# Selective scan: x_proj of a forward and its backward direction in one product, the result kept in DRAM, dt products contracted over all 108 rows

## The chip, the cores and the metric

The kernel runs on one core of one Trainium2 chip. The metric is the device time of one execution in microseconds; the time before is 4361.97 us, the median of three runs (4361.64 to 4367.63 us). The profile is one further execution, taken by the hardware profiler.

## The reference, cut to what matters

The model has two layers on an input of 4 images, 384 channels and 32 x 32 positions, all in fp32. Layer 0 is a selective scan (SSM) in four directions followed by a mixture of four experts, layer 1 is attention followed by a small feed-forward. The change touches the first lines of the scan alone:

```
xs = _cross_scan(x)          # k=0 rows, k=1 columns, k=2 rows reversed, k=3 columns reversed
x_dbl = einsum('bkdl,kcd->bkcl', xs, x_proj_weight)      # 44 x 384 for each k
dts, Bs, Cs = x_dbl[:, :, :12], x_dbl[:, :, 12:28], x_dbl[:, :, 28:]
dts = einsum('bkrl,kdr->bkdl', dts, dt_projs_weight)     # 384 x 12 for each k
dt = softplus(dts + bias)
h = h * exp(dt * A) + (dt * u) * B ;  y = sum_n h * C     # step by step along l
```

Directions 0 and 2 see the same positions in opposite order, and so do 1 and 3. The projection of a position does not depend on the order, so the x_dbl of directions k and k + 2 are two products over the same u.

## The kernel before, in words

Four images (b) are worked on one after another. Each image has eight units: the directions in the order 0, 1, 3, 2 (`ORDER`), and for each the two halves i of the 1024 steps, 512 at a time. The scan goes forward for k = 0 and 1 and backward for k = 2 and 3. Odd k are scanned along columns.

`project` (L292) prepares one unit. It loads `wdt` (L314), multiplies the normalized image u by x_proj in three products of 128 rows into 44 rows of PSUM (L317), copies the result to `xd` on ACT (L321), writes its rows 12 to 43 (B and C) to a DRAM tile `rows` (L323), and reads them back as four `bcs` tiles with each row spread over 32 partitions (L329). For odd k the moving operand of L317 is read column by column, with a step of 32 elements. Then, three times, `begin` forms dt: one product of `wdt` with the first 12 rows of `xd` (L344), five or six activations (L348 to L361), and for the first image four products by the identity (L357), for the others two subtractions on POOL (L374, L375) and an addition on DVE (L381). dt and dt x u go to the DRAM tile `dd` (L384, L385).

`chunk` (L388) does the scan of 128 channels of a unit; there are three in a unit, each in four groups g of four states. It reads `dd` back as `dtr` (L403), multiplies by B on POOL (L419, 24 in a unit), forms exp(dt x A) on ACT (L428, 48), scans on DVE (L433, 48), multiplies by C half on POOL (L447, 12) and half on DVE (L440, 24), and sums over the states in PSUM on PE (L454). The bx tiles are six (`bufs=6`), dtr seven, bcs five, and the working tiles `k2`, of which `wdt` and `xd` are two in each unit, six.

`scan_layer` runs `project` of the next unit, which is a generator, one step ahead between the groups of the current one. While the scan of image b runs, the rest of the network for image b - 1 (`tail_batch`: experts, attention, last layers) is put between its instructions. The order on each engine is not that of the source: `TileContext(schedule_with_timeline_sim=True)` lets a planner place every instruction, so a small edit can move all that follow. All ordinary loads and stores of the scan are issued from SP's queue, in its order.

What the change and the prediction touch: L192 (`wx`), L313 to L329 (the first part of `project`), L344 (the dt product), and in `layouts` the arrays `wx` and `wdt`.

Of the kernel before, what the change touches and what calls it, by code (L numbers as in the profile page):

```python
# [9 lines left out]
F32 = mybir.dt.float32  # L10
# [7 lines left out]
P = 128  # L18
B = 4
D = 384  # L20
DC = D // P
HW = 32
L = HW * HW
HF = 512
NH = L // HF

KG = 4
ORDER = (0, 1, 3, 2)
NS = 16
R = 12  # L30
XD = R + 2 * NS

NE = 4
TOP = 2
# [74 lines left out]
def halves(i):  # L109
    return slice(i * HF, (i + 1) * HF)  # L110


class Body:
# [68 lines left out]
    def scan_layer(self, x1, between):  # L182

        nc, tc, a = self.nc, self.tc, self.a
        with ExitStack() as ctx:
            wp = ctx.enter_context(tc.tile_pool(name="s_w", bufs=1))
            work = ctx.enter_context(tc.tile_pool(name="s_work", bufs=1))
            dram = ctx.enter_context(tc.tile_pool(name="s_dram", bufs=3, space=DRAM))
            dap = ctx.enter_context(tc.tile_pool(name="s_da", bufs=2, space=PSUM))
            psum = ctx.enter_context(tc.tile_pool(name="s_ps", bufs=2, space=PSUM))  # L190

            wx = wp.tile([P, DC, KG, XD], F32, tag="wx", name="wx")  # L192
            nc.scalar.dma_start(out=wx, in_=a["wx"].rearrange("(c p) k m -> p c k m", p=P))
            nega = wp.tile([P, KG * NB * NG], F32, tag="nega", name="nega")
            lo, hi = COL["alog"]
# [49 lines left out]
            us = {0: start(0)}  # L245
            ahead = []
            self.place_behind = None
            for _ in self.project(units[0], us[0], wx, work, dram, psum, ahead):
                pass
            self.layernorm(us[0], us[0], self.eps6, psum, work, parts=range(1, NH))  # L250
# [2 lines left out]
            for n, unit in enumerate(units):  # L253
                b, k, i = unit
# [12 lines left out]
                for c in range(DC):  # L267
# [5 lines left out]
                    if k % 2 == 0:  # L273
                        ys = y[:, c, halves(i)]
                        out = acc
                    else:
                        w = slice(i * (HW // NH), (i + 1) * (HW // NH))
                        ys = y[:, c, :].rearrange("p (h w) -> p h w", h=HW)[:, :, w]
                        out = acc.rearrange("p (w h) -> p h w", h=HW)
# [12 lines left out]
    def project(self, unit, u, wx, work, dram, psum, made):  # L292

        nc, a = self.nc, self.a
        b, k, i = unit
        by_cols = k % 2 == 1
        w = slice(i * (HW // NH), (i + 1) * (HW // NH))  # L300

        def part(c):
            if by_cols:
                return u[:, c, :].rearrange("p (h w) -> p w h", h=HW)[:, w, :]
            return u[:, c, halves(i)]

        def split(ap):
            return ap.rearrange("p (w h) -> p w h", h=HW) if by_cols else ap

        def k2(name, shape=(P, HF)):  # L310
            return work.tile([*shape], F32, tag="k2", name=name, bufs=6)

        wdt = k2("wdt", (R, D))  # L313
        nc.sync.dma_start(out=wdt, in_=a["wdt"][:, k, :])  # L314
        ps = psum.tile([P, HF], F32, tag="ps", name="xd_ps")
        for c in range(DC):
            nc.tensor.matmul(  # L317
                split(ps[:XD, :]), wx[:, c, k, :], part(c), start=(c == 0), stop=(c == DC - 1)
            )
        xd = k2("xd", (XD, HF))  # L320
        nc.scalar.copy(xd, ps[:XD, :])  # L321
        rows = dram.tile([2 * NS, HF], F32, tag="rows", name="rows")
        nc.sync.dma_start(out=rows, in_=xd[R:XD, :])  # L323
        view = rows.rearrange("(t g n) l -> n t g l", t=2, g=NG)
        bcs = []
        for g in range(NG):
            bc = work.tile([P, 2, HF], F32, tag="bcs", name="bcs", bufs=5)
            for n in range(NJ):
                nc.sync.dma_start(  # L329
                    out=bc[n * DB : (n + 1) * DB], in_=view[n, :, g].partition_broadcast(DB)  # L330
                )
            bcs.append(bc)

        dd = dram.tile([2, D, HF], F32, tag="dd", name="dd")
        made += [bcs, dd]
        yield  # L340

        def begin(c):
            ps = psum.tile([P, HF], F32, tag="ps", name="dt_ps")
            nc.tensor.matmul(ps, wdt[:, c * P : (c + 1) * P], xd[:R, :], start=True, stop=True)  # L344
            bias = self.col("dtb", k * DC + c)
            mag, one_e, lnw = k2("mag"), k2("one_e"), k2("lnw")
            relu = k2("relu") if b == 0 else ps
            nc.scalar.activation(mag, ps, AF.Abs, bias=bias)  # L348
            nc.scalar.activation(relu, ps, AF.Relu, bias=bias)
            nc.scalar.activation(mag, mag, AF.Exp, scale=-1.0)  # L350
            nc.scalar.activation(one_e, mag, AF.Identity, bias=1.0)
            nc.scalar.activation(lnw, one_e, AF.Ln)
            if b == 0:
                nc.scalar.activation(one_e, one_e, AF.Identity, bias=1.0, scale=-1.0)
                terms = [lnw, one_e, mag, relu]
                for t in terms:
                    nc.tensor.matmul(  # L357
                        ps, self.ident, t, start=(t is terms[0]), stop=(t is terms[-1])
                    )
            else:  # L360
                nc.scalar.activation(one_e, one_e, AF.Identity, bias=self.minus1)  # L361
            return ps, mag, one_e, lnw

        def behind(engine):
            if self.place_behind is None:
                return nullcontext()
            return self.tc.issue_after(self.place_behind[engine])

        for c in range(DC):
            ps, mag, one_e, lnw = begin(c)  # L370
            yield
            if b > 0:
                with behind("pool"):
                    nc.gpsimd.tensor_sub(mag, one_e, mag)  # L374
                    nc.gpsimd.tensor_sub(lnw, lnw, mag)  # L375
            yield
            d, du = mag, one_e
            rows = slice(c * P, (c + 1) * P)
            with behind("dve"):
                if b > 0:  # L380
                    nc.vector.tensor_add(ps, ps, lnw)  # L381
                nc.vector.tensor_mul(split(du), split(ps), part(c))
            nc.scalar.copy(d, ps)  # L383
            nc.sync.dma_start(out=dd[0, rows, :], in_=d)  # L384
            ins = nc.sync.dma_start(out=dd[1, rows, :], in_=du).ins  # L385
        made.append(ins)
# [968 lines left out]
def layouts(inputs):  # L1355

    i = {k: np.asarray(v) for k, v in inputs.items()}

    def vec(v, lead):
        return np.moveaxis(v.reshape(*lead, P, -1), len(lead), 0).reshape(P, -1)  # L1360

    packed = {
        "alog": np.ascontiguousarray(
            i["L0_conv_A_logs"].reshape(KG, NB, DB, NG, NJ).transpose(4, 2, 0, 1, 3)
        ).reshape(P, -1),
        "dtb": vec(i["L0_conv_dt_projs_bias"], (KG, DC)),
        "ds": vec(i["L0_conv_Ds"], (KG, DC)),
        "lnw": vec(i["L0_conv_ln_weight"], (DC,)),
        "lnb": vec(i["L0_conv_ln_bias"], (DC,)),
        "pj2": np.broadcast_to(i["L1_ffn_c_proj_2"].reshape(1, -1), (P, KJ)),  # L1370
        "c2": np.broadcast_to(i["L1_ffn_c_fc_2"].reshape(1, -1), (P, KJ)),
    }
    eye = np.repeat(np.eye(KR, dtype=np.float32), KJ, axis=0)
    nq = P // KR
    wout = i["L1_conv_w_out"].T.reshape(INNER // P, P, D)
    fc1 = i["L1_ffn_c_fc_1"].T
    arrays = {
        "x": i["x"].reshape(B, D, L),
        "cols": np.concatenate([packed[n] for n, _ in _COLS], axis=1),
        "wx": i["L0_conv_x_proj_weight"].transpose(2, 0, 1),  # L1380
        "wdt": i["L0_conv_dt_projs_weight"].transpose(2, 0, 1),
        "wg": i["L0_ffn_gate_w"],
        "bg": i["L0_ffn_gate_b"],
        "w1": i["L0_ffn_w1"].reshape(NE, DC, P, HID).transpose(0, 2, 1, 3),
        "w2": i["L0_ffn_w2"].reshape(NE, FC, P, D).transpose(0, 2, 1, 3),
        "bb": np.concatenate(
            [
                i["L0_ffn_b1"].reshape(NE, FC, P).transpose(0, 2, 1),
                np.broadcast_to(i["L0_ffn_b2"][:, None, :], (NE, P, D)),
            ],  # L1390
            axis=2,
        ),
        "wqkv": i["L1_conv_w_qkv"].T,
        "wa": wout[:-1].transpose(1, 0, 2).reshape(P, -1),
        "wb": np.concatenate(
            [
                wout[-1],
                np.broadcast_to(np.tile(i["L1_ffn_c_fc_2"].reshape(-1), KR), (P, D)),
                np.broadcast_to(i["L1_conv_b_out"], (P, D)),
            ],  # L1400
            axis=1,
        ),
        "wc": np.concatenate(
            [
                fc1.reshape(KR, FC // nq, nq, P).transpose(2, 0, 1, 3).reshape(P, -1),
                i["L1_ffn_c_proj_1"].T.reshape(FC, P, KR).transpose(1, 0, 2).reshape(P, -1),
                np.tile(eye.T, (nq, 1)),
            ],
            axis=1,
        ),  # L1410
    }
    return {k: np.ascontiguousarray(v) for k, v in arrays.items()}
# [16 lines left out]
```

## Time and profile before

| | us |
|---|---|
| median of the runs | 4361.97 |
| the profiled execution | 4365.25 |
| its span, first to last instruction | 4363.5 |
| first product of the scan on POOL (L419) starts | 43.8 |
| last product of the scan on POOL starts | 3518.9 |
| POOL, DVE, ACT, PE busy over the span | 3049.6, 2919.3, 2504.0, 3382.3 |
| x_proj products (L317): PE busy | 139.3 in 192 instructions |
| copies of x_proj's result (L321): ACT busy | 18.5 in 32 instructions |
| dt products (L344): PE busy | 123.2 in 192 instructions |

Of the span, the first 44 us fill the pipeline, some 3475 us are the 32 units of the scan with the other layers beside them, and the last 840 us are the remaining layers of the last image. One fp32 product stands as two instructions in the trace, so the three products of L317 are six. The profile names instructions by line, engine and tiles; "busy" is the time in which at least one instruction of an engine is at work, and after "idle before" comes what the engine waited for.

### The profile page before, as it was taken

Reading aid. Unit: us, or ns where it says so; the run is one execution under the profiler, and the core shown is the slowest. Engines: PE = TensorE matmul, PEld = TensorE weight load, DVE = VectorE, ACT = ScalarE, POOL = GpSimd, SP = SyncE. Lnnn points to the kernel's source line nnn. Section 1 sums busy time; section 2 is a strip of 40 time slices with the busy share of each in tenths; the row PEclk is TensorE's granted clock in tenths of the full one; section 3 lists DMA queues with packets and bytes.
Section 4 is the critical chain, followed back from the end, with each engine's and each line's share of the span. In section 5 each row is a group of like instructions: output and inputs, shape, how many; then the busy total and the mean of one; then the engine's idle time right before and its main releaser. Section 6 shows DMA issues by size and latency. Waiting matters only on the chain. (4 is left out here: it accounts for less than half of the span.)

```text
span 4363.5 us, 46084 instructions
## 1 busy us (share of the span) xinstructions
PE 3382.3 (78%) x13436; PEld 1581.3 (36%) x13436; DVE 2919.3 (67%) x4331; ACT 2504.0 (57%) x4470; POOL 3049.6 (70%) x1475
## 2 busy tenths in 40 slices
PE   6545544379997895579997888579998799999896
PEld 2111111145553221235554322135554234666323
DVE  5888888967877868968787867968887740200102
ACT  4445545556665875466575777466666564343353
POOL 5999998898988968688898978789898831000100
PEclk7766776589997997779998999679999899999997
DMA  5444354577886534457779534457789434336200
GB/s 136 114 122 116 106 162 115 151 228 214 231 241 183 142 109 139 125 174 213 213 229 279 154 95 132 115 158 225 215 233 273 134 108 142 116 126 214 63 17 15
DMA packets 404756, 684.74 MB, mean 157 GB/s; under 512 B 50960, under 2 KB 206480, under 8 KB 404496
## 3 DMA queue, kind: packets, MB, share of 16 engines
q1 hardware_dynamic: 395184, 655.37, 51.9%
q0 software_dynamic: 8192, 25.17, 1.7%
q8 instruction: 108, 1.77, 0.2%
q14 instruction: 152, 1.25, 0.1%
q10 hardware_dynamic: 1120, 1.18, 0.1%
HBM read 561.47 MB, written 120.06 MB: 156 GB/s over the span
## 5 line engine op out<-in xcount | busy, mean ns | idle before, releaser
L419 POOL TENSOR_TENSOR bx<-dtr,bcs 128x1024 f32<-128x1024 f32 x768 | 1792.4, 2361 | 229.6 <-PE acc L454 118.7
L428 ACT ACTIVATE da<-dtr,nega 128x512 f32<-128x512 f32 x1536 | 1045.3, 690 | 945.8 <-DVE bx L440 564.3
L447 POOL TENSOR_TENSOR bx<-bx,bcs 128x1024 f32<-128x1024 f32 x384 | 903.1, 2359 | 179.1 <-DVE carry L444 74.3
L906 PE MATMUL h_ps<-xc,w 128*128 128x256 f32 (+1 forms) x3168 | 675.0, 368 | 60.8 <-DMA w<-in_w 18.7
L454 PE MATMUL acc<-bx,sel 128*32 128x512 f32 x3072 | 496.8, 697 | 289.2 <-POOL bx L447 232.4
L921 PE MATMUL y_ps<-w,hs 128*128 128x384 f32 x1824 | 643.2, 505 | 38.1 <-ACT hs L914 37.8
L906 PEld LDWEIGHTS h_ps<-xc,w 128*128 128x128 f32 x3168 | 556.1, 200 | 238.7 <-issue 112.8
L433 DVE TENSOR_TENSOR_SCAN bx<-da,carry,bx 128x512 f32<-128x512 f32 x384 | 474.7, 1270 | 129.3 <-ACT da L428 65.8
L433 DVE TENSOR_TENSOR_SCAN bx<-da,bx 128x512 f32<-128x512 f32 x384 | 453.3, 1210 | 117.1 <-POOL bx L419 59.2
L433 DVE TENSOR_TENSOR_SCAN da<-da,carry,bx 128x512 f32<-128x512 f32 x384 | 478.0, 1274 | 66.5 <-ACT da L428 60.9
L440 DVE TENSOR_TENSOR bx<-da,bcs 128x512 f32<-128x512 f32 x768 | 510.3, 680 | 3.7
L433 DVE TENSOR_TENSOR_SCAN da<-da,bx 128x512 f32<-128x512 f32 x384 | 456.2, 1219 | 63.3 <-ACT da L428 53.0
L921 PEld LDWEIGHTS y_ps<-w,hs 128*128 128x128 f32 x1824 | 350.0, 196 | 325.8 <-issue 78.2
L1036 ACT ACTIVATE ex<-s_ps 128x512 f32<-128x512 f32 x512 | 300.8, 592 | 156.6 <-PE s_ps L1030 154.4
L1030 PE MATMUL s_ps<-w 64*128 64x512 f32 x1024 | 307.9, 662 | 53.1 <-ACT ex L1036 51.8
L911 ACT ACTIVATE hs<-h_ps,bb 128x256 f32<-128x256 f32 (+1 forms) x528 | 201.0, 441 | 218.8 <-PE h_ps L906 218.4
L1076 PE MATMUL o_acc<-ex,vt 128*64 128x512 f32 x1024 | 287.0, 638 | 18.1 <-ACT ex L1036 11.5
L454 PEld LDWEIGHTS acc<-bx,sel 128*32 128x32 f32 x3072 | 80.0, 116 | 585.9 <-POOL bx L447 319.8
L942 POOL TENSOR_TENSOR diag<-ident,g_weight 128x1024 f32<-128x1024 f32 x8 | 15.0, 1893 | 345.6 <-PE xc_ps L889 331.0
L925 DVE TENSOR_TENSOR y<-y_ps,bb 128x384 f32<-128x384 f32 x76 | 41.7, 549 | 273.4 <-PE y_ps L921 273.4
L344 PE MATMUL dt_ps<-xd,wdt 12*128 12x512 f32 x192 | 123.2, 726 | 71.4 <-ACT mag L383 43.8
L1030 PEld LDWEIGHTS s_ps<-w 64*128 64x128 f32 x1024 | 82.8, 190 | 256.0 <-ACT ex L1036 206.0
(214 smaller groups left out, 3767.2 us busy)
## 6 DMA issues: line engine op xcount, KB each, us to landing
w<-in_w SPq DMA_DIRECT2D x352, 576.0 KB
dtr<-dd SPq DMA_DIRECT2D x1536, 128.0 KB
bcs<-rows SPq DMA_DIRECT2D x512, 128.0 KB
dd<-one_e SPq DMA_DIRECT2D x96, 256.0 KB
dd<-mag SPq DMA_DIRECT2D x96, 256.0 KB
rows<-zero SPq DMA_DIRECT2D x76, 192.0 KB
xs<-rows SPq DMA_DIRECT2D x32, 384.0 KB
made<-y SPq DMA_DIRECT2D x32, 384.0 KB
```

The lines of the kernel that those rows point to most:

```text
L419: pool = nc.gpsimd.tensor_mul(bx, dtr[q][1], bc[:, 0].unsqueeze(1).to_broadcast([P, 2, HF])).ins
L428: nc.scalar.activation(da, dtr[q][0][:, j, :], AF.Exp, scale=nega[:, col : col + 1])
L433: nc.vector.tensor_tensor_scan(run(h), run(da), run(bx[:, j, :]), 0.0 if first else hold, ALU.mult, ALU.add,)
L440: dve = nc.vector.tensor_mul(bx[:, j, :], h, cg).ins
L447: pool = nc.gpsimd.tensor_mul(bx, bx, cg.unsqueeze(1).to_broadcast([P, 2, HF])).ins
L454: nc.tensor.matmul(acc[lo : lo + DB, :], sel, out[q][:, j, :], start=(g == 0), stop=(g == NG - 1),)
L906: nc.tensor.matmul(ps[:, r, :], w1[(f + r) // wf][:, c, (f + r) % wf * P : ((f + r) % wf + 1) * P], xc[:, c, :], start=(c == 0), stop=(c = ...
L911: nc.scalar.activation(hs[:, f + r, :], ps[:, r, :], AF.Identity, bias=bb[:, f + r : f + r + 1])
L921: nc.tensor.matmul(out[:, :D], hs[:, f, t * P : (t + 1) * P], w2[f // wf][:, f % wf, :], start=(f == 0), stop=(f == FC - 1),)
L1030: ins = nc.tensor.matmul(ps, w[rows, j * P : (j + 1) * P], w[rows, halves(i)], start=True, stop=True).ins
L1036: done.append(nc.scalar.activation(ex[:, o, :], ps, AF.Exp, scale=HD**-0.5, accum_out=sums[:, t, 2 * j + o, i : i + 1],).ins)
L1076: ins = nc.tensor.matmul(out[cols, :], made[t][1][:, j, cols], ex[:, o, :], start=(j == 0), stop=(j == MB - 1),).ins
```

## The change

The x_proj weights of k and k + 2 are put side by side in one stationary operand: columns 0 to 43 for k, columns 64 to 107 for k + 2, zeros between (`XA` = 64, `XP` = 108). For k = 0 and 1 one product gives both directions' rows, u is read in row order for both, and for k = 1 the result is written to PSUM in column order instead (`to_rows`). All 108 rows are copied to `xd` and stored in a DRAM tile `both`, one for each k and i. For k = 2 and 3 there is no product: `xd` is loaded from `both`. B and C are read from `both` at the rows of the direction. The dt product contracts over all 108 rows of `xd`, with a `wdt` that is zero outside the 12 rows of its direction.

```diff
-            wx = wp.tile([P, DC, KG, XD], F32, tag="wx", name="wx")
+            wx = wp.tile([P, DC, KG // 2, XP], F32, tag="wx", name="wx")
...
+            self.kept = {}
...
+        def rows_of(c):
+            if by_cols:
+                return u[:, c, :].rearrange("p (h w) -> p h w", h=HW)[:, :, w]
+            return u[:, c, halves(i)]
+
+        def to_rows(ap):
+            return ap.rearrange("p (w h) -> p h w", h=HW) if by_cols else ap
...
-        wdt = k2("wdt", (R, D))
-        nc.sync.dma_start(out=wdt, in_=a["wdt"][:, k, :])
-        ps = psum.tile([P, HF], F32, tag="ps", name="xd_ps")
-        for c in range(DC):
-            nc.tensor.matmul(
-                split(ps[:XD, :]), wx[:, c, k, :], part(c), start=(c == 0), stop=(c == DC - 1)
-            )
-        xd = k2("xd", (XD, HF))
-        nc.scalar.copy(xd, ps[:XD, :])
-        rows = dram.tile([2 * NS, HF], F32, tag="rows", name="rows")
-        nc.sync.dma_start(out=rows, in_=xd[R:XD, :])
+        wdt = k2("wdt", (XP, D))
+        nc.sync.dma_start(out=wdt, in_=a["wdt"][k])
+        xd = k2("xd", (XP, HF))
+        if k < KG // 2:
+            ps = psum.tile([P, HF], F32, tag="ps", name="xd_ps")
+            for c in range(DC):
+                nc.tensor.matmul(
+                    to_rows(ps[:XP, :]), wx[:, c, k, :], rows_of(c),
+                    start=(c == 0), stop=(c == DC - 1),
+                )
+            nc.scalar.copy(xd, ps[:XP, :])
+            both = dram.tile([XP, HF], F32, tag=f"both{k}{i}", name="both")
+            nc.sync.dma_start(out=both, in_=xd)
+            self.kept[k, i] = both
+        else:
+            both = self.kept[k - KG // 2, i]
+            nc.sync.dma_start(out=xd, in_=both)
+        at = k // (KG // 2) * XA + R
+        rows = both[at : at + 2 * NS, :]
...
-            nc.tensor.matmul(ps, wdt[:, c * P : (c + 1) * P], xd[:R, :], start=True, stop=True)
+            nc.tensor.matmul(ps, wdt[:, c * P : (c + 1) * P], xd, start=True, stop=True)
...
+    wx = np.zeros((D, KG // 2, XP), np.float32)
+    wdt = np.zeros((KG, XP, D), np.float32)
+    for k in range(KG):
+        at = k // (KG // 2) * XA
+        wx[:, k % (KG // 2), at : at + XD] = i["L0_conv_x_proj_weight"][k].T
+        wdt[k, at : at + R] = i["L0_conv_dt_projs_weight"][k].T
```

More of the change, by code (lines that the diff above doesn't have):

```diff
@@ L31 @@
 XD = R + 2 * NS
+XA = P // 2
+XP = XA + XD
 NE = 4
@@ L1379, in layouts @@
         "cols": np.concatenate([packed[n] for n, _ in _COLS], axis=1),
-        "wx": i["L0_conv_x_proj_weight"].transpose(2, 0, 1),
-        "wdt": i["L0_conv_dt_projs_weight"].transpose(2, 0, 1),
+        "wx": wx,
+        "wdt": wdt,
         "wg": i["L0_ffn_gate_w"],
```

## The prediction

> **What bounds the kernel now.** I read the page's slices first, then a table of stages, then the timeline of the projection itself. The slices (tenths of busy time, granted TensorE clock under them) show three regimes.
>
> ```profile
> PE   6545544379997895579997888579998799999896
> ...
> DVE  5888888967877868968787867968887740200102
> ...
> POOL 5999998898988968688898978789898831000100
> PEclk7766776589997997779998999679999899999997
> ```
>
> In slices 1 to 6 (the first image's scan, nothing beside it) POOL is at nine tenths, DVE at eight, PE at five. In later slices the experts of the image before run beside the scan and PE rises to nine. In the last eight slices only PE works. The table by stage gives sizes; after the window and its length come busy us of PE, PEld, DVE, ACT, POOL, then the clock, the DMA share and GB/s.
>
> ```profile
> 43.80:663.00 619.20, 331.40 (x940) 82.76 (x940) 546.77 (x745) 316.81 (x498) 583.27 (x253) 0.70 0.47 125
> ...
> 909.30:1333.90 424.60, 395.99 (x1675) 235.28 (x1673) 337.49 (x456) 274.91 (x441) 364.41 (x169) 0.95 0.80 230
> ...
> 1945.30:2368.80 423.50, 393.44 (x1671) 235.04 (x1670) 338.15 (x458) 276.63 (x438) 364.67 (x169) 0.96 0.79 230
> ...
> 2875.40:3292.20 416.80, 376.44 (x1562) 219.81 (x1561) 339.34 (x457) 274.20 (x423) 364.50 (x169) 0.94 0.73 208
> ...
> 3521.00:4363.50 842.50, 754.65 (x3179) 395.60 (x3175) 109.63 (x296) 365.29 (x779) 51.72 (x40) 0.94 0.31 103
> ```
>
> Row 1 is the first image's seven units: POOL 583.3 of 619.2, so 35.9 us idle, 5.1 a unit, and no change here can gain more while its 36 products a unit (583.3 / 7 = 83.3 us) stay. Rows 2 to 4 are the expert stretches, four units each: PE has 29, 30 and 40 us idle, POOL 60, 59 and 52, so PE is the nearer limit. The last row holds no projection. The operation concerned, in the groups by shape and in the timeline of PE:
>
> ```profile
> L317 PE MATMUL xd_ps<-u,wx 128*44 128x512 f32 x192 | 139.3, 869 | 16.8 <-DVE y L281 7.4 <-DVE u L178 4.8 <-DVE y L285 3.0
> ```
>
> ```profile
> 1120.23 5.33 PE L317 MATMUL xd_ps<-u,wx 128*44 128x512 f32 x6
> ```
>
> ```profile
> 2374.55 2.77 PE L317 MATMUL xd_ps<-u,wx 128*44 128x512 f32 x6 [0.96 <-ACT mag L383]
> ```
>
> The six instructions of one projection take 5.33 us when u is read by columns and 2.77 by rows. Last, who waits for it:
>
> ```profile
>   ACT xd L321: 34.0, 15
> ```
>
> ACT stood 34.0 us, in 15 of 32 units, with its copy at the head of its queue and the scan's exponentials (L428) behind it.
>
> **What the Trainium skill says.** "SBUF — State Buffer", under "Door 1: The DMA port swizzle", gives SBUF lines of 16 bytes: an access that enters a new line each time pays. The trace agrees: 128-byte steps cost 5.33 against 2.77. "PSUM — Partial Sum Buffer", "Specifications (TRN2)", says any non-contiguous pattern slows matmuls significantly; no product in this trace writes PSUM with steps. "TensorE: Matmul & The Clock Gate", "LDWEIGHTS", says a weight load goes by columns, not contracted rows, and its "Step-by-step" that streaming takes N cycles; the trace agrees: the dt product of 12 rows has a minimum of 587 ns, the projection of 128 rows 592. "DMA: Bandwidth & Descriptors", "Why a DMA increments its semaphore by 16 and not by 1", says a DMA takes the largest number of engines up to 16 that divides its outer dimension, 12 for 108 rows; no run here shows it.
>
> **Part by part.** There are 8 projections of each direction (4 images, 2 halves).
>
> *Removed products (k = 2, 3).* 8 x 5.33 + 8 x 2.77 = 64.8 us of PE. What counts is where. From the PE timeline, each expert stretch holds two for k = 3 and one for k = 2: 2 x 5.33 + 2.77 = 13.4, three times 40.3 us. PE is busy 93, 93 and 90% there, but its order interleaves products that wait for POOL and ACT, and shortening it shifts the wait to them; I take 0.6: **24 us**. The other 24.5 us lie where PE is at five to eight tenths: nothing by themselves. Their cover is POOL's products.
>
> *Removed copies.* 16 copies of 0.578 us and the waits before them; those of k = 2 and 3 sum from the ACT timeline to 19.1 us, 8.8 of them in the first image. There ACT is held 8.8 + 4 x 0.58 = 11.1 us. DVE waits for the exponentials, POOL for DVE, and both have slack (72 and 36 us over seven units); I take a third: **4 us**. In the expert stretches this is inside the 0.6.
>
> *Row order for k = 1.* u is read in runs of 16, but PSUM is written with a step of 32. Bounds: 2.77 (the write is free, 8 x 2.56 = 20.5 us of PE saved) and 10.7 (the step costs as much again). I take 5.33: **0**. The weight load grows from 44 to 108 columns (116 ns at least, to the 200 of 128 columns, L906) and is pulled ahead of the running product: 0, at worst 48 x 2 x 0.08 = 8 us.
>
> *dt products over 108 rows.* Same streaming, same 128 columns: 0; without that, 192 instructions would have to lengthen by 45 ns to cost 8.7 us.
>
> *DRAM.* Stores: 16 of 221 KB for 32 of 66 KB. Loads: 16 of 221 KB new, `wdt` 166 KB for 18, 32 times. Together +9.7 MB on 684.7, 1.4%. The expert stretches run at 0.73 to 0.80 DMA share: a fifth is free, and 1.25 MB more at 230 GB/s over 0.80 is 4.3 us of all engines each, mostly hidden; charged **2 us** in all, bounds 0 and 13.
>
> *SP's queue.* The load of `xd` stands right behind that of `wdt` in most units, a queue slot that waited for a `k2` tile already; behind it wait `dtr` reads, which POOL needs. In the built program its first dt product stands one to three groups of sums later (8 to 30 us). No dt product waits for `wdt` in the trace of before, from nearly the same place, so I charge 0. If a weight load of the experts ahead of it in the queue delays it, the dt product blocks PE, and with it the sums that free the bx tiles: 16 loads, 5 us each at worst.
>
> *The new order.* The planner moved everything after the first product. In the built program POOL's order in the first image was mostly AAAAAACCC (A is L419, C is L447): six tiles filled, then three multiplications by C. Now it is AAC, each C two or more A behind its own. A group needs two A and one C, 3 x 2.31 = 6.9 us on POOL; a C has two A = 4.6 us for the two scans before it (2.44 in DVE's timeline), so DVE may be 2.2 us late. DVE's group (four scans 4.9, two products 1.27, also from there) fits within 6.9. Five buffers of six are used, so POOL's waits for the sums (15.7 us in this image) should shrink, and DVE adds to y behind two scans instead of ahead of them. Of the 35.9 us idle I expect a third less beside the 4 above; with care: **5 us**. In later images the order changes without a direction I can read.
>
> *Start and end.* The first store is 155 KB longer, ahead of the first loads in SP's queue: 1 us at most. After the scan's last sum four more score products and two more table loads (1.28 us each) remain than before: **4 us** with the start.
>
> Sum: 24 + 4 + 5 - 2 - 4 = **27 us** less. The profiled execution took 4365.25 (span 4363.5 and 1.75 around), 3.3 above the median of the runs, 4361.97; from its own time 4338, and from the median, which is what will be compared, **4335**. A change of 0.2% is 8.7 us, about what a measurement of this kernel can tell from none.
>
> **Rivals.**
> 1. *PE's time counts in full.* All 40.3 us return, the stepped PSUM write is free (4 of its 8 places lie in expert stretches: 10 us), and the first image gives 20: 4362 - 40 - 10 - 20 + 6 = 4298. For it: 90 to 93% PE there. Against: POOL at 86% and DVE at 80% in the same windows, with waits on each other.
> 2. *Hidden anyway.* POOL's chain sets every unit, and PE's time comes out of its idle shares: 9 less 6, so 4359. For it: POOL's longest waits in the first expert stretch are for DVE (19 us of 50 in all), for dtr (13) and for ACT (11), for the sums of PE only 12.
> 3. *Slower: the tight order.* The place is C (L447), 12 in each unit of the first image and in the like patterns later. With C two A behind, any lateness of DVE over 2.2 us (a dt product 0.86, an addition to y 0.68, 16 carry copies of 0.15 a chunk in the first half of a direction) stops POOL at once, where six filled tiles used to cover it. The price is 84 times the mean wait in seven units; today's waits for DVE there are 12.7 us. A mean of 0.43 us (36 us) eats the 27 and 8.7 more: from there it is slower. At 0.6 us it is 50 us, so 4362 - 27 + 50 = 4385. Against: DVE is at 547 of 619.
> 4. *Slower by PSUM steps* is the same sign and less likely: each k = 1 projection would have to take about 14 us, beyond my bound.
>
> That the change doesn't do what it says is excluded by the built program: 48 projection products for 96, and 16 loads of `xd`.
>
> **Chances.** Forecast 0.40, rival 1 0.20, rival 2 0.16, slower order or a like loss at the image changes 0.24. The first two are faster, so faster 0.60; rival 2 is "same", 0.16; slower 0.24. The range has to reach both ends: low 4290 (rival 1 with 8 us more), high 4385 (rival 3), beyond each about one in ten. The faster cases alone span 4290 to 4352.
>
> **What would show it.** Expert stretches shorter by 5 to 12 us each at equal POOL busy time: the removed products. First image: seven units at 86 us instead of 88.5, with fewer waits of POOL for sums. Projections for k = 1 at 5.3 us: the PSUM write costs what the read did; 2.8 would say it is free. dt products at a minimum near 590 ns. No wait on DMA of `xd`. Wrong would be: POOL's waits for DVE in the first image above 36 us, dt products longer than before, or PE waiting for `xd`; or a gain lying in the changes of image, which I priced at nothing.

## The result, and the profile after

The changed kernel takes 4340.47 us in the median of 7 runs (4336.28 to 4351.74), the kernel before 4361.97 (7 runs, 4353.58 to 4367.63): a ratio of 0.9957, 95% interval 0.9946 to 0.9968, or 21.5 us less. The prediction said 27 less. The profiled execution took 4344.16 us, with a span of 4342.4, so the two profiled spans differ by 21.1 us and can be compared stage by stage.

The slices of the changed kernel, in the order of those shown of before:

```profile
PE   6444454398987885679986887569987889998896
...
DVE  5999997887787868878886778967877730200101
...
POOL 5999997798888968789998688778988820000100
PEclk8666666599998996789998999779998899999897
```

The regimes are the same. In slices 1 to 5 DVE has risen from eight tenths to nine, and PE is a tenth lower in three of them: the same work of the scan is packed closer, with less of PE beside it (298 us in the first image, 331 before). The table of stages (window, length, then busy us of PE, PEld, DVE, ACT, POOL, clock, DMA share, GB/s): the first image, the three expert stretches, and the tail after the last POOL product of the scan has begun.

```profile
44.20:636.90 592.70, 298.17 (x917) 76.66 (x916) 544.75 (x745) 316.86 (x495) 582.43 (x253) 0.68 0.52 135
886.30:1297.00 410.70, 374.96 (x1661) 235.16 (x1659) 336.39 (x458) 271.52 (x436) 363.13 (x169) 0.96 0.81 235
1900.20:2302.40 402.20, 372.14 (x1658) 233.82 (x1659) 339.67 (x460) 268.94 (x427) 365.53 (x171) 0.97 0.85 237
2812.70:3252.80 440.10, 377.04 (x1603) 223.00 (x1600) 338.61 (x460) 292.64 (x444) 378.49 (x183) 0.91 0.73 207
3485.00:4342.40 857.40, 765.92 (x3203) 399.07 (x3203) 113.21 (x299) 370.65 (x786) 53.90 (x40) 0.93 0.31 102
```

Row 1: 592.7 where it was 619.2, with the same POOL work (582.4 against 583.3). POOL's idle time has gone from 35.9 us to 10.3. Rows 2 and 3 are 13.9 and 21.3 us shorter, row 4 is 23.3 longer, although all three lost products. By stage, before and after. A unit is taken to start at every 36th of POOL's products (24 by B and 12 by C a unit):

| stage | before | after | difference |
|---|---|---|---|
| start | 43.8 | 44.2 | +0.4 |
| first image, units 0 to 6 | 619.2 | 592.7 | -26.5 |
| units 7, 8 | 246.3 | 249.4 | +3.1 |
| units 9 to 12, experts | 424.6 | 410.7 | -13.9 |
| units 13 to 17 | 611.4 | 603.2 | -8.2 |
| units 18 to 21, experts | 423.5 | 402.2 | -21.3 |
| units 22 to 25 | 506.6 | 510.3 | +3.7 |
| units 26 to 29, experts | 416.8 | 440.1 | +23.3 |
| units 30, 31 | 226.7 | 232.2 | +5.5 |
| tail | 844.6 | 857.4 | +12.8 |

So the first image gives 26.5 us, everything from unit 7 to the end of the scan only 7.8 together, and the tail takes 12.8 back. The total is close to the forecast and nearly every part of it is not.

The operations themselves: the projection in the groups by shape, six of its instructions for k = 1 (read by rows, written to PSUM by columns) in the timeline of PE, the dt product under its tile, and ACT's wait for the projection.

```profile
L330 PE MATMUL xd_ps<-u,wx 128*108 128x512 f32 x96 | 59.7, 772 | 12.6 <-DVE u L180 7.5 <-ACT mag L402 2.7 <-DVE y L284 2.3
```

```profile
890.85 2.74 PE L330 MATMUL xd_ps<-u,wx 128*108 128x512 f32 x6
```

```profile
L363 PE MATMUL dt_ps<-xd,wdt x192: 590/594/1223, 22.7 to 3336.6; 108*128 108x512 f32 x192
...
  ACT xd L334: 7.6, 5
```

Projections: 59.7 us of PE for 139.3. The k = 1 projection takes 2.74 us, as a row-read one does (2.77): the stepped PSUM write costs nothing. A dt product over 108 rows is at 590 ns at least, where 12 rows were at 587. ACT waits 7.6 us in 5 units, for 34.0 in 15. These prices came out as hoped; what they were worth in time did not follow from them.

### The profile page after: what moved, and what is told of

Same layout as the page of the kernel before. It is cut to its first block, busy times and chain, and to the rows that moved or that the text cites. A ratio compares the mean times of both kernels' runs of the same rounds, so it can differ in the third digit from the quotient of the medians.

```text
span 4342.4 us, 45822 instructions
## 1 busy us (share of the span) xinstructions
PE 3303.7 (76%) x13340; PEld 1577.5 (36%) x13340; DVE 2915.6 (67%) x4331; ACT 2504.3 (58%) x4460; POOL 3049.3 (70%) x1475
## 5 line engine op out<-in xcount | busy, mean ns | idle before, releaser
L438 POOL TENSOR_TENSOR bx<-dtr,bcs 128x1024 f32<-128x1024 f32 x768 | 1795.1, 2364 | 216.2 <-PE acc L473 103.2
L466 POOL TENSOR_TENSOR bx<-bx,bcs 128x1024 f32<-128x1024 f32 x384 | 905.2, 2362 | 160.3 <-DVE carry L463 67.3
L925 PE MATMUL h_ps<-xc,w 128*128 128x256 f32 (+1 forms) x3168 | 659.5, 363 | 52.0 <-DMA w<-in_w 27.0
L363 PE MATMUL dt_ps<-xd,wdt 108*128 108x512 f32 x192 | 123.9, 732 | 73.3 <-ACT mag L402 43.9
```

Source lines behind the costliest of these rows:

```text
L438: pool = nc.gpsimd.tensor_mul(bx, dtr[q][1], bc[:, 0].unsqueeze(1).to_broadcast([P, 2, HF])).ins
L466: pool = nc.gpsimd.tensor_mul(bx, bx, cg.unsqueeze(1).to_broadcast([P, 2, HF])).ins
L925: nc.tensor.matmul(ps[:, r, :], w1[(f + r) // wf][:, c, (f + r) % wf * P : ((f + r) % wf + 1) * P], xc[:, c, :], start=(c == 0), stop=(c = ...
```

## The experiments

My theory after the result: two things were mixed. Shorter products on PE pay in the expert stretches at some fixed share; and the planner, given any changed instruction, may write another order, which in the first image alone is worth 26 us. Rivals: the first image gains because the copies on ACT are gone; or the gain is the removed products after all and the stages only shift. An edit that changes only an access pattern leaves the order of every engine as it was (in the traces of the five such pairs, no more than one or two pairs of instructions of an engine change places); an edit that changes a shape or a tile does not. The first kind prices PE time in a fixed order, the second shows what an order is worth. The numbers for all kernels, each beside the kernel before on the same chip. The stages come from one profiled execution each; it lies 17 us above its kernel's median for reuse_alone, 12 below for slow_dt_after, and within 6 for the others:

| kernel | median | ratio, 95% | first image | unit 7 to scan end | tail |
|---|---|---|---|---|---|
| before | | | 619.2 | 2855.9 | 844.6 |
| after | 4340.47 | 0.9957, 0.9946 to 0.9968 | 592.7 | 2848.1 | 857.4 |
| rows_read | 4344.13 | 0.9960, 0.9946 to 0.9973 | 616.2 | 2838.9 | 841.2 |
| cols_read | 4339.03 | 0.9945, 0.9931 to 0.9960 | 592.1 | 2855.2 | 852.1 |
| dt44 | 4307.13 | 0.9870, 0.9853 to 0.9888 | 591.3 | 2822.3 | 852.1 |
| dt44_rows | 4290.36 | 0.9841, 0.9827 to 0.9854 | 591.5 | 2797.7 | 852.3 |
| wdt44_load | 4378.35 | 1.0038, 1.0024 to 1.0052 | 619.3 | 2838.3 | 879.0 |
| bx5 | 4347.96 | 0.9968, 0.9956 to 0.9980 | 592.4 | 2877.2 | 836.7 |
| reuse_alone | 4309.12 | 0.9872, 0.9856 to 0.9888 | 589.7 | 2848.2 | 844.2 |
| reuse_dt12 | 4310.59 | 0.9885, 0.9870 to 0.9900 | 590.8 | 2837.8 | 839.8 |
| slow_dt_before | 4371.95 | 1.0036, 1.0023 to 1.0049 | 619.2 | 2866.3 | 840.7 |
| slow_dt_after | 4346.27 | 0.9970, 0.9958 to 0.9982 | 597.8 | 2838.7 | 852.1 |

### rows_read: PE time taken out in the order of before

The kernel before, with u of k = 1 and 3 read in rows and the result written to PSUM in columns. No product is removed, and all engines keep their order.

```diff
-                split(ps[:XD, :]), wx[:, c, k, :], part(c), start=(c == 0), stop=(c == DC - 1)
+                to_rows(ps[:XD, :]), wx[:, c, k, :], rows_of(c), start=(c == 0), stop=(c == DC - 1)
```

> The kernel before with one edit: x_proj of the column directions (k = 1 and 3) reads u in row order and writes PSUM in column order. The planner gives every engine the same order as before, so only the real time of 16 projections changes, 5.33 to 2.8 us each, 41 us of PE in all, 26 of them in the expert stretches. If PE's time counts at 0.6 there (the prediction's step): about 16 us less than before, 4346. If the gain of the change came from the order and PE's time is nearly hidden: 0 to 5 us less, 4357 to 4362.

Measured: 0.9960 (0.9946 to 0.9973), 16 us less by the medians. The three expert stretches and the projection under its line:

```profile
905.80:1319.60 413.80, 383.54 (x1675) 233.18 (x1673) 337.06 (x455) 274.38 (x441) 364.27 (x169) 0.96 0.80 235
1931.70:2351.60 419.90, 384.32 (x1670) 234.09 (x1669) 337.73 (x457) 276.79 (x438) 364.53 (x170) 0.96 0.80 233
2858.50:3271.40 412.90, 371.47 (x1561) 220.19 (x1561) 338.99 (x457) 274.39 (x423) 364.32 (x169) 0.93 0.73 209
```

```profile
L325 PE MATMUL xd_ps<-u,wx x192: 592/592/1082, 17.8 to 3281.0; 128*44 128x512 f32 x192
```

The stretches are 10.8, 3.6 and 3.9 us shorter, 18.3 in all. They hold ten projections that became 2.56 us shorter (5.33 less 2.77), 25.6 us: a price of 0.7 for a microsecond of PE there, in this order. The two profiled executions lie 23.7 us apart, though, where the medians lie 16 apart. If all of the medians' difference (12 to 24 us by the interval) is put down to the stretches, the price is 0.6, between 0.5 and 0.9. The first image moved 3 us. The median product is 592 ns, equal to the minimum, so stepped writing costs nothing against 1035 ns (the median of this group in before) for the same product in 96 of whose instructions u was read in steps.

### cols_read: the same in the order of after, the other way

The changed kernel, with u of k = 1 read by columns again and PSUM written in a row. Same order as the changed kernel.

```diff
-                    to_rows(ps[:XP, :]), wx[:, c, k, :], rows_of(c),
+                    split(ps[:XP, :]), wx[:, c, k, :], part(c),
```

> The changed kernel with x_proj of k = 1 reading u by columns again and writing PSUM in a row; same order on every engine as the changed kernel. 8 projections of 5.33 instead of 2.8 us, 20 us more PE, four of them in the expert stretches. PE at 0.6: 6 us slower than the changed kernel, 4346. PE hidden: within 2 us of it, 4340 to 4342.

Measured: 0.9945 (0.9931 to 0.9960), against 0.9957 of the changed kernel: no loss. Eight projections grew by 2.56 us, some 10 us of it in the expert stretches, and these moved by +0.9, +1.8 and -2.5 us. By the 0.7 of rows_read it should have been about 7 longer; the two intervals together put it between 13 us shorter and 3 longer. The row order for k = 1 is thus worth nothing that these runs resolve in this order of the kernel; why the price isn't the same in both orders stays open.

### dt44: an edit that removes nothing

The kernel before, with the dt product contracted over all 44 rows of `xd` and zeros in `wdt` for the 32 rows of B and C. All 96 projections and all copies stay.

```diff
-        wdt = k2("wdt", (R, D))
-        nc.sync.dma_start(out=wdt, in_=a["wdt"][:, k, :])
+        wdt = k2("wdt", (XD, D))
+        nc.sync.dma_start(out=wdt, in_=a["wdt"][k])
...
-            nc.tensor.matmul(ps, wdt[:, c * P : (c + 1) * P], xd[:R, :], start=True, stop=True)
+            nc.tensor.matmul(ps, wdt[:, c * P : (c + 1) * P], xd, start=True, stop=True)
```

> The kernel before with one edit: the dt product contracts over all 44 rows of xd, with a wdt of 44 rows that is zero below the 12th. All 32 projections stay, by columns where they were. On the chip this adds nothing but 50 KB to each load of wdt; the planner's order changes, and POOL's order in the first image is that of the changed kernel. If the order makes the gain: the first image's units take 83 to 84 us instead of 88, 26 us less in all, 4336, give or take 15 us from the later images, whose order changes too. If removed PE time makes it: 4362, with units of 86 to 88 us.

Measured: 0.9870 (0.9853 to 0.9888), 53 us less, more than twice what the change itself gives. I had expected 4336, give or take 15, from the order; 4307 is 14 below that range, and the excess lies behind the first image. The first image and the projections:

```profile
42.50:633.80 591.30, 313.27 (x940) 78.57 (x940) 544.08 (x745) 318.48 (x499) 582.79 (x253) 0.68 0.51 132
```

```profile
L317 PE MATMUL xd_ps<-u,wx 128*44 128x512 f32 x192 | 138.2, 865 | 30.9 <-ACT mag L383 24.6 <-DVE u L178 4.7 <-DVE y L281 1.0
```

PE still spends 138.2 us on projections (139.3 before), and the first image takes 591.3 us, as in the changed kernel. So the 26.5 us of the first image need neither the removed products nor the removed copies. What differs is the order. POOL in before, in the first image (start, length, line, tiles, count):

```profile
312.29 13.87 POOL L419 TENSOR_TENSOR bx<-dtr,bcs 128x1024 f32<-128x1024 f32 x6
326.11 4.66 POOL L447 TENSOR_TENSOR bx<-bx,bcs 128x1024 f32<-128x1024 f32 x2
331.07 2.35 POOL L447 TENSOR_TENSOR bx<-bx,bcs 128x1024 f32<-128x1024 f32 x1 [0.30 <-DVE bx L433]
...
359.33 11.60 POOL L419 TENSOR_TENSOR bx<-dtr,bcs 128x1024 f32<-128x1024 f32 x5 [3.49 <-PE acc L454]
```

and in the changed kernel, where the same two lines are L438 and L466:

```profile
310.71 2.34 POOL L466 TENSOR_TENSOR bx<-bx,bcs 128x1024 f32<-128x1024 f32 x1
313.01 4.65 POOL L438 TENSOR_TENSOR bx<-dtr,bcs 128x1024 f32<-128x1024 f32 x2
317.63 2.33 POOL L466 TENSOR_TENSOR bx<-bx,bcs 128x1024 f32<-128x1024 f32 x1
319.93 4.68 POOL L438 TENSOR_TENSOR bx<-dtr,bcs 128x1024 f32<-128x1024 f32 x2
```

Before, six products by B fill all six bx tiles in a burst, three products by C follow, and so on; of the bursts shown, the third stands still until PE's sums free a tile (the 3.49 us in brackets; the second stands in the lines left out). In the changed kernel two and one alternate. The waits of POOL in the first image from its second unit on (for whom, us, times, longest), of before, from 136.1 to 663:

```profile
POOL bx L419 <- PE acc L454: 15.7, 8, 4.0
...
POOL bx L447 <- DVE bx L433: 4.9, 5, 1.6
POOL bx L447 <- DVE carry L444: 4.2, 5, 1.5
```

and of the changed kernel, from 135.2 to 636.9:

```profile
POOL bx L438 <- issue: 1.0, 1, 1.0
POOL bx L438 <- POOL bx L466: 0.8, 1, 0.8
POOL bx L438 <- DMA dtr<-dd: 0.8, 1, 0.8
```

Both kinds of waits, for PE's sums and for DVE's scans, are gone from these six units. In the first unit 7.7 us of waits for DVE are left. In dt44, in its own six units, POOL's products wait for nothing.

### wdt44_load: the load without the rows

dt44, but the product reads only the first 12 rows again; what is left of the edit is the larger load of `wdt` (66 KB for 18).

```diff
-            nc.tensor.matmul(ps, wdt[:, c * P : (c + 1) * P], xd, start=True, stop=True)
+            nc.tensor.matmul(ps, wdt[:R, c * P : (c + 1) * P], xd[:R, :], start=True, stop=True)
```

> The kernel before with wdt loaded with 44 rows, 32 of them zero, and the dt product still over 12: the other half of dt44. In the built program the order of the first ten units on POOL is that of before, and later ones differ. If the order sets the first image: its seven units at 87 to 88 us as before, and the rest off from before by up to 20 us either way, 4342 to 4382. If the larger load made dt44 faster: 83 to 84 us a unit there.

Measured: 1.0038 (1.0024 to 1.0052), 17 us slower than before. The first image and the tail:

```profile
43.80:663.10 619.30, 331.79 (x941) 82.88 (x940) 546.90 (x745) 316.90 (x498) 583.08 (x253) 0.70 0.47 126
```

```profile
3501.42:4380.40 878.98, 798.47 (x3359) 404.39 (x3357) 114.08 (x301) 388.97 (x851) 53.89 (x40) 0.94 0.29 98
```

The first image is that of before to 0.1 us, with POOL's order of before (bursts): the larger load costs nothing there. From unit 7 on the order is another one: the scan ends 17.6 us earlier, but 3359 instructions are then left on PE, for 3191 in the same stretch of before, and the tail is 34.4 us longer. An order that runs the scan ahead of the other layers has to pay for them at the end, so neither part may be read alone. How much of the 17 us is order, and whether the load has a part in it behind the first image, isn't shown.

### bx5: the burst made impossible

The kernel before with five bx tiles for six, and nothing else. A burst of six can't be written.

```diff
-                bx = work.tile([P, 2, HF], F32, tag="bx", name="bx", bufs=6)
+                bx = work.tile([P, 2, HF], F32, tag="bx", name="bx", bufs=5)
```

> The kernel before with five bx tiles for six, all else as it is. POOL's order becomes C A A throughout the first image's units: one multiplication by C after each two by B. If what held POOL there is the burst order, in which six tiles fill and then wait for the sums of PE: 83 to 85 us a unit with a tile less, 15 to 30 us less in the first image, the rest off by up to 20 us either way, 4315 to 4365. If what held it is the number of tiles: 90 us a unit or more, 4375 and up.

Measured: 0.9968 (0.9956 to 0.9980), 13 us less with a buffer less. The first image:

```profile
41.70:634.10 592.40, 332.19 (x941) 78.86 (x940) 544.33 (x741) 314.37 (x497) 582.46 (x252) 0.68 0.48 132
```

592.4 us, with all projections, all copies and 12-row dt products. After the first unit POOL's order is one product by C and two by B in turn, and this is all that POOL's products wait for from the second unit on (133.5 to 634.1):

```profile
POOL bx L447 <- DVE bx L433: 1.5, 1, 1.5
```

A tile less can by itself only make POOL wait longer for a free one, so the order is what the first image gains from. The other engines' orders changed along with POOL's, here and in dt44, and no run changes POOL's alone. That the order acts through POOL's waits is read from the traces: 15.7 us for the sums in before, none in this kernel. From unit 7 on, this kernel lost 13.4 us against before (2877.2 and 836.7 for 2855.9 and 844.6); whether by its order or by the missing tile isn't shown.

### reuse_alone and reuse_dt12: the change without its 108-row products

reuse_alone is the changed kernel with dt over 12 rows, `wdt` as before, and for k = 2 and 3 a load of only the 12 dt rows of `both`.

```diff
+        wdt = k2("wdt", (R, D))
+        nc.sync.dma_start(out=wdt, in_=a["wdt"][:, k, :])
...
+            xd = k2("xd", (R, HF))
+            nc.sync.dma_start(out=xd, in_=both[XA : XA + R, :])
...
+            nc.tensor.matmul(ps, wdt[:, c * P : (c + 1) * P], xd[:R, :], start=True, stop=True)
```

reuse_dt12 keeps the 108-row tiles and the full load of `xd`, and loads and contracts only the 12 rows of the direction.

```diff
+        lo = k // (KG // 2) * XA
+        nc.sync.dma_start(out=wdt[lo : lo + R, :], in_=a["wdt"][k][lo : lo + R, :])
...
+            nc.tensor.matmul(
+                ps, wdt[lo : lo + R, c * P : (c + 1) * P], xd[lo : lo + R, :],
+                start=True, stop=True,
+            )
```

> The changed kernel with dt over 12 rows as before: wdt of 12 rows, and for k = 2 and 3 only the 12 rows of dt are loaded from DRAM into xd. The products are as few as in the changed kernel, 48 fewer than before. The order is a third one, with the first image's POOL order of the changed kernel. If removed PE time makes the gain: 4335 to 4340, as the changed kernel. If the order makes it: first image's units at 83 to 84 us, and the later images off by up to 15 us either way from the changed kernel, 4325 to 4355.

> The changed kernel with the dt product over the 12 rows of its direction (rows 0 to 11 or 64 to 75 of xd) and only those 12 rows of wdt loaded; xd is still loaded with 108 rows. As many products as in the changed kernel and in reuse_alone, a further order. If the number of products sets the time: as the changed kernel, 4340. If the order does: first image at 83 to 84 us a unit, the total anywhere from 4305 to 4345.

Measured: 0.9872 (0.9856 to 0.9888) and 0.9885 (0.9870 to 0.9900). Both are 30 to 37 us faster than the changed kernel by the ratios, both have the alternating order and a first image of 590 us. (For reuse_alone I had expected 4325 at the least; it took 4309.) Nearly all of the difference lies behind the first image. A dt product over 108 rows is not slower than one over 12 (590 ns and 587 at least), so it isn't the product itself. Two causes are left: each of these kernels has an order of its own from unit 7 on, and the changed kernel, unlike these two, loads 166 KB of `wdt` for each unit. No run tells them apart. What the two kernels do show is that the reuse, too, brings the planner to the alternating order in the first image, as the wider dt product does.

### dt44_rows: the parts that paid, together

dt44 with the edit of rows_read, which keeps dt44's order.

```diff
+                to_rows(ps[:XD, :]), wx[:, c, k, :], rows_of(c), start=(c == 0), stop=(c == DC - 1)
...
+            nc.tensor.matmul(ps, wdt[:, c * P : (c + 1) * P], xd, start=True, stop=True)
```

> dt44 (the kernel before, dt over 44 rows) with x_proj of k = 1 and 3 read in row order and written to PSUM in column order. Same order on every engine as dt44, 41 us less PE, 10 of the 16 projections in or beside the expert stretches. If removed PE time counts there at 0.6 to 0.7, as the pair before and rows_read says: 13 to 18 us less than dt44, 4290 to 4294. If it counts for nothing, as the pair of the changed kernel and cols_read says: 4305 to 4309.

Measured: 0.9841 (0.9827 to 0.9854), 4290.36 us: the best of all, 71 us below the kernel before and, by the ratios, some 50 below the changed kernel. Against dt44 it is 16.8 us less by the medians, which come from two chips, and 12.6 by the ratios; rows_read was 16 less than before. So the price of PE time repeats in a second fixed order, as far as the noise lets it be seen. It removes no projection.

### slow_dt_before and slow_dt_after: PE time put in

The dt product with its streams read and written in steps of 32, with the same result and the same order, in the kernel before and in the changed one.

```diff
+            cols = "p (w h) -> p h w"
+            nc.tensor.matmul(
+                ps.rearrange(cols, h=HW), wdt[:, c * P : (c + 1) * P],
+                xd[:R, :].rearrange(cols, h=HW), start=True, stop=True,
+            )
```

(In the changed kernel `xd` stands for `xd[:R, :]`.)

> The kernel before with each dt product reading its moving operand with a step of 32 elements and writing PSUM with the same step, so that the result is the same and each of the 192 instructions takes about 0.43 us longer: 82 us more PE, 2.6 in every unit; same order on every engine. With the price that rows_read showed, 0.7 in the expert stretches (10.3 us added in each of three) and 0.2 to 0.3 elsewhere: 7 us longer in each stretch, 30 to 35 in all, 4392 to 4397. If PE's time is hidden: under 10 in all.

> The changed kernel with its dt products slowed in the same way, 82 us more PE in its own order. If PE's price is the same in its order: 7 us longer in each expert stretch, 30 to 35 in all, 4371 to 4376. If PE is no longer near the path there, as cols_read hints: 0 to 3 us a stretch, 5 to 15 in all, 4345 to 4355.

Measured: 1.0036 (1.0023 to 1.0049), 13.7 us more, where I had expected 30 to 35; and 0.9970 (0.9958 to 0.9982), about 6 us above the 0.9957 of the changed kernel, with intervals that overlap. The dt products of slow_dt_before, in the groups by shape:

```profile
L345 PE MATMUL dt_ps<-xd,wdt 12*128 12x512 f32 x192 | 189.7, 1076 | 71.6 <-ACT mag L387 44.1 <-DVE y L285 12.5 <-DVE y L281 12.4
```

189.7 us for 123.2: 66.5 us of PE added, 13.7 of time. In each of the three expert stretches the 12 dt products (24 instructions) took 10.1 us more (23.6 for 13.4), 30.4 in all, and the stretches moved by -0.1, +4.5 and +4.5: a price of 0.3. But here the profiled executions lie 3.9 us apart where the medians lie 13.7 apart. With all of the medians' difference (10 to 21 us by the interval) put down to the stretches, it is 0.5, between 0.3 and 0.7. This overlaps with the 0.5 to 0.9 of the projections: both groups are worth less than their time, and whether their prices differ isn't shown. My expectation failed either in the 0.7 or in the 0.2 to 0.3 that it gave to the rest of the program. The first image, where PE is at half, didn't move at all (619.2); in the alternating order of slow_dt_after it was 5 us longer (597.8 for 592.7, one execution each).

## Why the prediction was right in the total and wrong in its parts

*The removed products (24).* Half right. The 0.6 taken for PE time in the expert stretches was near: rows_read gave 0.6 by the medians and 0.7 by the stages, in before's order. By it, 40.3 us of removed products would be 24 to 28. In the order of the changed kernel cols_read showed no price. What either says of removed products is an inference, since no run removed products with the order kept. But from unit 7 to the end of the scan the kernel gained 7.8 us, and with the tail it lost 5.0. The step failed where it used one window's price and left the rest of the order neutral ("in later images the order changes without a direction I can read", priced at 0). Nothing I had read gave that term a sign, but it should have widened the working. Four kernels with the work of before (before, wdt44_load, bx5, and dt44, which adds only rows to the contraction) take 3700.5, 3717.3, 3713.9 and 3674.4 us from unit 7 to the end: 43 us apart without a projection removed. The three with reuse (after, reuse_alone, reuse_dt12) take 3705.5, 3692.4 and 3677.6, on average 10 less than those four, which is inside their spread (14 less, and 42 apart, when each is moved to its kernel's median). What the reuse alone is worth is therefore not settled. That this change's later order gave back what its products saved is an inference from the price, not a measurement.

*The third expert stretch.* The prediction had it 5 to 12 us shorter; it was 23.3 longer. In the changed kernel 16 scatters of expert rows on POOL's queue moved from unit 25 to 26, and units 25, 26 and 27 took 130.1, 130.3 and 109.0 us for 142.8, 110.2 and 96.8; POOL's instructions in the window rose from 169 to 183. wdt44_load shows the same move and the same stretch (439.9). That the scatters are the cause was not tried by themselves.

*The new order in the first image (5), with the copies (4).* This is the term that failed most: 26.5 for 9. I had read the order right (AAAAAACCC before, AAC after) and had argued the direction right, fewer waits for the sums, but expected a third of the idle time and charged 5 us of it "with care", where seven tenths came back. The sign that the prediction named, 86 us a unit, was already worth 17 us, twice what its sum charged. A unit went from 88.5 to 84.7 us, with POOL's own 83.3 as its floor. The copies have no visible part: dt44 and bx5 keep all of them and are at 591.3 and 592.4. That the gain is the order's is shown by bx5 and dt44, which remove nothing, and by wdt44_load, which keeps the bursts and gains nothing: all four kernels with bursts lie at 616 to 619 us, all eight with an alternating order at 590 to 598.

*Row order for k = 1 (0).* The cost was at the low bound: 2.74 us, no price for the step in PSUM. "PSUM — Partial Sum Buffer", "Specifications (TRN2)", in the Trainium skill says any non-contiguous pattern slows matmuls significantly; for this fp32 product of 512 columns the measurement says no, 592 ns stepped and in a row, and the measurement decides. In time it was still 0 (cols_read), for a reason other than mine. Rival 4's 14 us a projection are not worked out: at PE's full price 9.8 would have been enough to undo the 27 us and 8.7 more, and that is inside the bound of 10.7. The 2.74 settles it all the same.

*dt over 108 rows (0), SP's queue (0), DRAM (2).* The minimum stayed (590 ns for 587). The prediction's numbers for this are of the streaming alone; the weight loads go by columns too: 184 ns in the median for 12 rows of 128 columns, 190 for 108 rows, 120 and 178 for 128 rows of 44 and 108 columns. The longer load of the projections, charged with 0, cost nothing that shows: six instructions take 2.74 us, and 91 of the 96 loads began while a product ran. No wait for a load of `xd` shows on PE, and the DMA traffic grew by 9.75 MB, as reckoned. But what is loaded behind them was waited for longer: from unit 7 to the end of the scan ACT waited 31.2 us for `dtr` (13.1 before) and PE 33.5 for the experts' weights (13.7). Such waits come without wide loads too: rows_read, with the loads and the order of before, has 28.8 for the weights, and reuse_dt12, with 12 rows of `wdt`, 28.0 for `dtr`. So the runs neither charge the wide loads with a time nor clear them; a run with wide loads in an order kept would, and there is none.

*Start and end (4).* 13.2 measured, 0.4 at the start and 12.8 in the tail. I had counted four score products and two table loads left over behind the scan. In the trace the score products are as many as before (444 instructions), but twelve more instructions of another attention product (`w_ps`, 72 for 60) are left, some 8 us of PE, and two more table loads of 1.28 us on ACT. PE is busy 9.6 us longer in the tail (765.9 for 756.3). The rest has not been traced.

*The rivals.* The tight order (rival 3) has the sign wrong: with two products by B behind each product by C, POOL's waits for DVE did not rise from 12.7 us but fell to 7.7, all in the first unit. "PE in full" (rival 1) fell with the total and with prices below 1, though two of its parts came true: the free PSUM write, and 20 us or more in the first image. "Hidden anyway" (rival 2) is nearest for the removed products as the kernel stands, and it had no room for an order worth 26 us.

In one sentence: an error of +17.5 us in the first image, of 14 the other way between unit 7 and the scan's end (7.8 for 22, DRAM's 2 taken off the 24), and of 9 in start and tail nearly cancelled, so that the close total is luck.

## What to carry to other kernels

Where a planner places every instruction, an edit is two changes: its work and a new order. Price the work with an edit that the planner doesn't see (an access pattern, not a shape), compare the kernels by stages that begin and end at the same unit, and count a scan that ends early together with the tail that it leaves. Before crediting a gain to removed work, try a harmless edit of the same place (a buffer less, rows of zeros): here one that removed nothing gave 53 us, and the change 21.5.

## What the runs showed of the hardware beyond expectation

An fp32 product that writes PSUM with a step of 128 bytes takes what a contiguous one takes (592 ns, 2.74 us for six), while one that reads its moving operand with that step takes twice as long (5.33 us for six): so in this kernel a transposition that a product must make is cheaper on its output. Contracting over 12, 44 or 108 rows made next to no difference to the streaming (587 ns at least for 12 and 44, 590 for 108). And with PE at 90 to 93%, a microsecond of PE was worth less than a microsecond: 0.3 to 0.9 us by the intervals of two edits in the order of before, and nothing that could be resolved for the projections in the order of the changed kernel.
